# Casts of edge indices on ScalarE, sums cleared group by group, and a shorter Newton step in the head of a graph kernel

## The chip, the cores and the metric

The kernel runs on one core of one Trainium2 chip. The metric is the device time of one execution in microseconds (us). Engines are named as in the profile: PE (TensorE), DVE (VectorE), ACT (ScalarE), POOL (GpSimd), SP (SyncE, which here only issues DMAs).

## The reference

Two layers work on x, 12500 rows of 256. The first is a graph layer with 200000 edges, sorted by target; the second is graph attention with 131072 edges and a mixture of four experts.

```python
z = layernorm(x)
x = x + segment_sum(z[src] * edge_weight[:, None], dst) @ W.T + b
y = layernorm(x)
x = x + moe(y, scores=gat(y, edge_index))
```

LayerNorm is (x - mean) / sqrt(var + 1e-5) without scale and shift in the first layer.

## The kernel before

The 12500 rows are 98 tiles of 128 (NT); groups of 4 tiles (GT) make 25 groups (NG), the last of which has 2. The part that the change touches is the head, everything ahead of the loop over edges:

- Constants, then POOL clears acc_x, 99 tiles of 256 columns in which the sums of the first layer are collected, in 33 pieces of 3 tiles (L162, L163).
- SP loads src, dst and edge_weight as rows of 128 edges (L185 to L194, 1664 columns on each of 128 partitions with the rest row), then the first six groups of x (L213). The pool of x buffers has six (L171), so the load of a group must wait until the store of the group six before it has landed.
- `turned` (L196) turns each of the three so that an edge's chunk is a column: integers are first cast to float in place on DVE (L199), then 13 PE transposes in pieces of four into PSUM (L205), each piece copied out by ACT (L207). src goes to src1, dst to dst_f, the weights to w1.
- `windows` (L235 to L294) works out from dst_f which tiles of targets each window of 768 edges reaches, and splits the second layer's edge indices. It is some 30 instructions of DVE with a few of PE, and is called in the code when the statistics of group 8 have been issued.
- The LayerNorm loop (L298 to L316): for group g the statistics (L104, L105), var + EPS (L111) on DVE and the square root on ACT (L112); and for the group before, the Newton step that refines 1/root (L118 to L122, DVE), the offset -mean*r (L311, DVE), the normalisation of the tiles in place on ACT (L314), and the store to z_rows from ACT's queue (L316).
- W is loaded, turned on PE and ACT and stored (L321 to L328), all from memory that the x buffers and the head's scratch had; and L329 copies the first 5120 columns of the cleared acc_x to gat_starts, which thereby starts as zeros.

Then comes the loop over 261 windows (L581 to L605): POOL gathers 128 rows of z for each of 1563 chunks of edges (L550), DVE makes one-hot matrices, ACT scales them by w1 (L556), PE multiplies them with the gathered rows (L564), and DVE adds a window's sums to acc_x (L571). Beside it a counting sort of the second layer's edges runs on PE, DVE and ACT. The order of that loop is written out by hand for PE, DVE and ACT. In the head the framework puts the instructions of each engine in order, and not always in that of the code: in the trace L329 is issued ahead of all loads of x but the first six, and each store of z behind the first normalising instruction of the next group.

The Newton step of before, which the change rewrites, is

```python
nc.vector.reciprocal(r, s)
nc.vector.tensor_mul(s, r, r)
nc.vector.tensor_mul(s, s, v)
nc.vector.tensor_scalar(s, s, -0.5, 1.5, ALU.mult, ALU.add)
nc.vector.tensor_mul(r, r, s)
```

with v = var + EPS and s its root, cut to the tiles of the group.

Of the kernel before, what the change touches and what calls it, by code (L numbers as in the profile page):

```python
# [23 lines left out]
F32 = mybir.dt.float32  # L24
# [4 lines left out]
AF = mybir.ActivationFunctionType  # L29
ALU = mybir.AluOpType  # L30
# [4 lines left out]
P = 128  # L35
N, D = 12500, 256
NT = 98
# [15 lines left out]
GT = 4  # L53
NG = (NT + GT - 1) // GT
LOW = -1.0e30
CODE = 8192
EPS = 1e-5
# [3 lines left out]
def gnn_gat_moe(ctx, tc, x, src, dst, edge_weight, W, b, W_gat, att_src, att_dst, b_gat, ln_gamma,  # L61
                ln_beta, W1, b1, W2, b2, edge_index, out):
    nc = tc.nc
# [10 lines left out]
    def after_all(ins, others):  # L74

        for o in others:
            tc.add_manual_dep(ins.ins, o.ins.name, mybir.DependencyInfo(
                mybir.DependencyClass.Sync, mybir.DependencyReason.DATA),
                reason="one wait for what the next ones read")

    def rows_of(g):
        t0 = g * GT
        n = min(GT, NT - t0)
        return t0, n, min(N, (t0 + n) * P) - t0 * P

    def node_rows(table, t0, n):
        return table[t0 * P:(t0 + n) * P, :].rearrange("(t p) d -> p t d", p=P)

    def load_x(pool, g, eng):
        t0, n, rows = rows_of(g)  # L90
        full = rows // P
        xt = pool.tile([P, GT, D], F32, name="xt")
        eng.dma_start(xt[:, :full, :], node_rows(x, t0, full))
        if full < n:
            nc.vector.memset(xt[64:P, full, :], 0.0)
            eng.dma_start(xt[:TAIL, full, :], x[(t0 + full) * P:N, :])
        return xt

    def statistics(pool, xt, n):

        st = pool.tile([P, GT, 6], F32, name="st")
        mv = pool.tile([P, GT, 2], F32, name="mv")
        for i in range(n):
            nc.vector.bn_stats(st[:, i, :], xt[:, i, :])  # L104
            nc.vector.bn_aggr(mv[:, i, :], st[:, i, :])  # L105
        return mv, root(pool, mv[:, :n, 1], [P, GT], n)

    def root(pool, var, shape, n):
        v = pool.tile(shape, F32, name="v_eps")
        s = pool.tile(shape, F32, name="root")  # L110
        nc.vector.tensor_scalar_add(v[:, :n], var, EPS)  # L111
        nc.scalar.activation(s[:, :n], v[:, :n], AF.Sqrt)  # L112
        return v, s

    def rooted(pool, v, s, shape, n):

        r = pool.tile(shape, F32, name="rstd")
        nc.vector.reciprocal(r[:, :n], s[:, :n])  # L118
        nc.vector.tensor_mul(s[:, :n], r[:, :n], r[:, :n])
        nc.vector.tensor_mul(s[:, :n], s[:, :n], v[:, :n])  # L120
        nc.vector.tensor_scalar(s[:, :n], s[:, :n], -0.5, 1.5, ALU.mult, ALU.add)
        nc.vector.tensor_mul(r[:, :n], r[:, :n], s[:, :n])  # L122
        return r
# [35 lines left out]

    wide = tc.alloc_tile_pool(name="wide", bufs=1)  # L160
    acc_x = wide.tile([P, NT + 1, D], F32, name="acc_x")
    for k in range(0, NT + 1, 3):  # L162
        nc.gpsimd.memset(acc_x[:, k:k + 3, :], 0.0)  # L163
    with ExitStack() as s1:
        edges = s1.enter_context(tc.tile_pool(name="edges", bufs=1))
        small = s1.enter_context(tc.tile_pool(name="small", bufs=2))
# [18 lines left out]
        def chunk_load(ap, dt, name):  # L185
            t = prep.tile([P, full + 1, P], dt, name=name)
            nc.vector.memset(t[:, full, :], 0)
            nc.sync.dma_start(t[:, :full, :],
                              ap[0:full * P * P].rearrange("(k r e) -> r k e", r=P, e=P))
            at = full * P * P  # L190
            nc.sync.dma_start(t[:rest, full, :],
                              ap[at:at + rest * P].rearrange("(r e) -> r e", e=P))
            nc.sync.dma_start(t[rest:rest + 1, full, 0:left], ap[at + rest * P:E][None, :])
            return t  # L194

        def turned(t, into):  # L196
            if t.dtype != F32:
                f = t.bitcast(F32)
                nc.vector.tensor_copy(f, t)  # L199
                t = f  # L200
            for k0 in range(0, full + 1, GT):
                n = min(GT, full + 1 - k0)
                pp = ps.tile([P, GT, P], F32, name="look")
                for k in range(n):
                    nc.tensor.transpose(pp[:, k, :], t[:, k0 + k, :], ident)  # L205
                m = min(n * P, NQ * GQ - k0 * P)
                nc.scalar.activation(into[:, k0 * P:k0 * P + m],  # L207
                                     pp.rearrange("p k e -> p (k e)")[:, :m], AF.Copy)

        rows = [chunk_load(ap, dt, f"rows{k}") for k, (ap, dt) in enumerate(  # L210
            ((src, I32), (dst, I32), (edge_weight, F32)))]
        XB = 6
        early = [load_x(xp, g, nc.sync) for g in range(XB)]  # L213
        src1 = edges.tile([P, NQ * GQ], I32, name="src1")
        dst_f = prep.tile([P, NQ * GQ], F32, name="dst_f")
        w1 = edges.tile([P, NQ * GQ], F32, name="w1")
        for t, to in zip(rows, (src1, dst_f, w1)):
            turned(t, to)
        dst2 = prep.tile([P, NC2], I32, name="rows0")
        nc.sync.dma_start(dst2, edge_index[1].rearrange("(p c) -> p c", c=NC2))  # L220
        src2 = prep.tile([P, NC2], I32, name="rows2")
# [75 lines left out]
        ahead = None  # L297
        for g in range(NG + 1):  # L298
            done = ahead
            if g < NG:  # L300
                xt = early[g] if g < XB else load_x(xp, g, nc.sync)
                ahead = (g, xt, *statistics(small, xt, rows_of(g)[1]))
            if g == XB + 2:
                windows()
            if done is None:
                continue
            was, xt, mv, vs = done
            t0, n, _ = rows_of(was)
            r = rooted(small, *vs, [P, GT], n)
            off = small.tile([P, GT], F32, name="off")  # L310
            nc.vector.scalar_tensor_tensor(off[:, :n], mv[:, :n, 0], -1.0, r[:, :n], ALU.mult,  # L311
                                           ALU.mult)
            for i in range(n):
                nc.scalar.activation(xt[:, i, :], xt[:, i, :], AF.Identity, bias=off[:, i:i + 1],  # L314
                                     scale=r[:, i:i + 1])
            nc.scalar.dma_start(node_rows(Z, t0, n), xt[:, :n, :])  # L316
        sx.close()

        turning = s0.enter_context(tc.tile_pool(name="turning", bufs=1, reuse_waits="tile"))
# [240 lines left out]
        def product(rows, hots, there):  # L560

            win = ps.tile([P, D], F32, name="win")
            for j, (r, h) in enumerate(zip(rows, hots)):
                i = nc.tensor.matmul(win, h, r, start=(j == 0), stop=(j == len(rows) - 1))  # L564
                if j == 0:
                    after_all(i, there)
            return win
# [5 lines left out]
        def group(q):  # L573
            return prepare(src1, lo_q, w1, [c for c in range(q * GQ, (q + 1) * GQ) if c * P < E])
# [3 lines left out]
        with tc.manual_schedule(engines={mybir.EngineType.PE, mybir.EngineType.DVE,  # L578
                                         mybir.EngineType.Activation}):
            at, done, coming, win = (), 0, group(0), None  # L580
            for q in range(NQ + 1):  # L581
                was, win = win, product(*coming) if q < NQ else None
# [9 lines left out]
                if q < NQ and q % 4 == 0:  # L592
                    n = min(4, NQ - q)
# [3 lines left out]
                for work, q0, q1, steps in parts:  # L597
                    if q == q0:
                        done = 0
# [14 lines left out]
        with tc.If(further > 0):  # L614
# [9 lines left out]
            with tc.For_i(0, NQ, 1) as q:  # L624
                nc.vector.memset(shift, 0.0)
                n = nc.values_load(more[0:1, bass.ds(q, 1)], min_val=0, max_val=NT,
                                   skip_runtime_bounds_check_because=BOUND)
# [29 lines left out]
    with ExitStack() as s2:  # L657
        gp = s2.enter_context(tc.tile_pool(name="gp", bufs=3))
        small = s2.enter_context(tc.tile_pool(name="small2", bufs=3))
# [124 lines left out]
    with ExitStack() as s3:  # L784
# [20 lines left out]
        turned = []  # L805
# [52 lines left out]
        t = pre.tile([P, L2], F32, name="scan")  # L858
# [151 lines left out]
        def joined(m_in, s_in, m_own, name):  # L1010

            m = tail.tile([P, H], F32, name="m_" + name)
            nc.vector.tensor_max(m, m_in, m_own)
            f = tail.tile([P, 2, H], F32, name="f_" + name)
            nc.vector.tensor_sub(f[:, 0, :], m0, m)
            nc.vector.tensor_sub(f[:, 1, :], m_own, m)
            nc.scalar.activation(f, f, AF.Exp)
            return m, f
# [12 lines left out]
        _, f = joined(m_in, None, end[:, NS:], "end")  # L1031
# [13 lines left out]
        m, f = joined(m0, None, row[:, NS:], "row")  # L1045
# [7 lines left out]
    with ExitStack() as s4:  # L1053
# [118 lines left out]
        g, last = 0, None  # L1172
        for t0, t1 in ((0, 12), (12, 36), (36, 80), (80, NT)):
            with tc.issue_after(last.ins) if last else ExitStack():
                gates(t0, t1 - t0)
            while g * GT < t1:
                last = mixed(g)
# [26 lines left out]
```

## Time and profile before

| what | us |
|---|---|
| median of three runs | 4193.42 (4192.93 to 4193.94) |
| the profiled execution | 4198.22 |
| its span | 4196.4 |
| first root of LayerNorm (ACT) | 37.04 |
| first store of z (ACT's queue) | 41.76 |
| last store of z | 130.27 |
| first gather (POOL) | 141.18 |

Busy shares over the whole span: PE 85%, POOL 69%, DVE 57%, ACT 34%. The timeline lists instructions in order of their start, with duration, engine, line of the code, tiles written and read, and in brackets the idle time ahead of one and what ended it; SPq and ACTq are the queues from which SP and ACT issue DMAs, and equal neighbours are drawn together with their count. The stretches view gives busy time by engine between two points in time, then the granted PE clock, the DMA share and GB/s.

| stretch, us | DVE busy | ACT busy | POOL busy | DMA share | GB/s |
|---|---|---|---|---|---|
| 0 to 25 | 19.66 | 1.29 | 24.39 | 0.75 | 222 |
| 25 to 35 | 7.03 | 4.74 | 0.00 | 0.18 | 52 |
| 35 to 60 | 22.72 | 15.20 | 0.00 | 0.81 | 277 |
| 60 to 80 | 17.81 | 10.64 | 0.00 | 0.76 | 249 |
| 80 to 100 | 13.35 | 10.12 | 0.00 | 0.81 | 269 |
| 118 to 140 | 8.51 | 12.13 | 0.00 | 0.54 | 181 |

### The profile page before, as it was taken

Reading aid. Unit: us, or ns where it says so; the run is one execution under the profiler, and the core shown is the slowest. Engines: PE = TensorE matmul, PEld = TensorE weight load, DVE = VectorE, ACT = ScalarE, POOL = GpSimd, SP = SyncE. Lnnn points to the kernel's source line nnn. Section 1 sums busy time; section 2 is a strip of 40 time slices with the busy share of each in tenths; the row PEclk is TensorE's granted clock in tenths of the full one; section 3 lists DMA queues with packets and bytes.
Section 4 is the critical chain, followed back from the end, with each engine's and each line's share of the span. In section 5 each row is a group of like instructions: output and inputs, shape, how many; then the busy total and the mean of one; then the engine's idle time right before and its main releaser. Section 6 shows DMA issues by size and latency. Waiting matters only on the chain. (4 is left out here: it accounts for less than half of the span.)

```text
span 4196.4 us, 54596 instructions
## 1 busy us (share of the span) xinstructions
PE 3552.0 (85%) x18969; PEld 2610.1 (62%) x18970; DVE 2393.0 (57%) x5474; ACT 1421.4 (34%) x3289; POOL 2906.0 (69%) x2855
## 2 busy tenths in 40 slices
PE   1466899999999999999998959999989999899545
PEld 0365676767766667767677836666656666566424
DVE  7566777878787878787778950221211202212477
ACT  4322445445545444545452211221212212212122
POOL 2577777777777777777776777777777777773440
PEclk6688999999999999999999969999999999999767
DMA  7433333333333333333335652222222222221698
GB/s 234 135 93 93 102 102 100 100 100 101 100 101 100 99 101 101 100 101 100 99 102 157 191 145 60 67 72 55 64 50 75 75 55 64 65 60 62 206 226 346
DMA packets 265845, 457.42 MB, mean 109 GB/s; under 512 B 67943, under 2 KB 168705, under 8 KB 264289
## 3 DMA queue, kind: packets, MB, share of 16 engines
q0 software_dynamic: 114128, 219.11, 21.4%
q1 hardware_dynamic: 111663, 207.52, 14.0%
q10 hardware_dynamic: 39778, 27.28, 2.1%
q8 instruction: 153, 2.51, 0.2%
q14 instruction: 123, 1.01, 0.1%
HBM read 334.05 MB, written 119.66 MB: 108 GB/s over the span
## 5 line engine op out<-in xcount | busy, mean ns | idle before, releaser
L550 POOL DMA_INDIRECT gt<-z_rows,src x1563 | 1605.2, 1027 | 592.2 <-issue 410.2
L809 POOL DMA_INDIRECT G<-gat_nodes,order x1024 | 1026.5, 1002 | 339.3 <-issue 289.0
L564 PE MATMUL win<-gt,oh_w 128*128 128x256 f32 x3126 | 770.1, 398 | 200.4 <-DMA gt<-z_rows,src 149.3
L564 PEld LDWEIGHTS win<-gt,oh_w 128*128 128x128 f32 x3126 | 598.0, 198 | 317.0 <-issue 188.4
L966 PE MATMUL po<-w,hh 128*128 128x256 f32 x3136 | 724.3, 385 | 51.4 <-ACT hh L948 38.3
L966 PEld LDWEIGHTS po<-w,hh 128*128 128x128 f32 x3136 | 605.5, 193 | 220.8 <-issue 87.1
L970 DVE TENSOR_TENSOR fo<-po,b 128x512 f32<-128x512 f32 x196 | 135.3, 690 | 1016.6 <-PE po L966 1016.6
L942 PE MATMUL ph<-yt,w 128*128 128x512 f32 (+1 forms) x1600 | 707.8, 586 | 2.8 <-DMA w<-in_L_ffn_W 2.8
L556 ACT ACTIVATE oh_w<-hit_w,w 128x128 f32<-128x128 bf16 x1563 | 500.9, 390 | 448.2 <-PE win L564 226.6
L490 DVE TENSOR_SCALAR st<-along,place_l,code 128x1024 bf16<-128x1024 f16 x1024 | 550.3, 578 | 162.3 <-PE perm L498 161.7
L948 ACT ACTIVATE hh<-ph,b 128x512 f32<-128x512 f32 (+1 forms) x400 | 249.3, 676 | 1001.6 <-PE ph L942 1001.5
L498 PE MATMUL perm<-st,to_p 128*128 128x512 bf16 x2048 | 524.1, 378 | 0.0
L942 PEld LDWEIGHTS ph<-yt,w 128*128 128x128 f32 x1600 | 305.0, 191 | 292.5 <-issue 277.9
L454 PE MATMUL look<-next,oht 98*128 98x128 f32 x2044 | 393.8, 300 | 0.0
L454 PEld LDWEIGHTS look<-next,oht 98*128 98x128 f32 x2044 | 309.6, 192 | 37.5
L462 ACT ACTIVATE next<-place 98x256 f32<-98x256 f32 x511 | 196.1, 384 | 345.1 <-PE place L459 344.3
L469 DVE TENSOR_TENSOR sel<-look,oh_lo 128x512 f32<-128x512 f32 x256 | 174.9, 683 | 186.4 <-PE look L454 185.2
L498 PEld LDWEIGHTS <-to_p 128*128 128x128 bf16 x2048 | 178.5, 97 | 122.3 <-DVE st L490 0.4
L571 DVE SCALAR_TENSOR_TENSOR acc_x<-win,in,acc_x 128x256 f32 x522 | 246.9, 473 | 8.7 <-PE win L564 8.6
L450 PE MATMUL look<-oh_lo,same_hi 128*128 128x128 bf16 x1024 | 228.1, 223 | 1.2 <-ACT next L462 1.0
L442 ACT ACTIVATE same_hi<-bank 128x512 bf16<-128x512 f32 x256 | 152.8, 597 | 215.2 <-PE bank L440 215.1
L340 DVE TENSOR_TENSOR oh_hi<-twice,hi 128x784 bf16<-128x784 bf16 x256 | 143.4, 560 | 100.6 <-PE place L364 100.5
(278 smaller groups left out, 3641.8 us busy)
## 6 DMA issues: line engine op xcount, KB each, us to landing
expert_rows<-fo SPq DMA_DIRECT2D x48, 1024.0 KB, 4.2
fo_in<-expert_rows SPq DMA_DIRECT2D x24, 2048.0 KB, 16.4
gt<-z_rows,src POOLq DMA_INDIRECT x1563
G<-gat_nodes,order POOLq DMA_INDIRECT x1024
xt<-in_x SPq DMA_DIRECT2D x24, 512.0 KB, 4.8
z_rows<-xt ACTq DMA_DIRECT2D x24, 512.0 KB, 4.6
x_two<-in_x SPq DMA_DIRECT2D x12, 1024.0 KB, 6.4
x_rows<-x_two SPq DMA_DIRECT2D x12, 1024.0 KB, 10.6
```

The source lines that it names most:

```text
L450: first = nc.tensor.matmul(look[:, i % GT + k, :], b["m"][:, i + k, :], one(b["ol"], i + k), start=True, stop=False)
L454: nc.tensor.matmul(look[:, i % GT + k, :], b["oht"][:, i + k, :], nxt[:, k, :], start=False, stop=True)
L490: last = nc.vector.tensor_scalar(st[:, k, :], along, b["l"][:, i + k:i + k + 1], code2[:, c:c + 1], ALU.is_equal, ALU.mult)
L498: first = nc.tensor.matmul(perm[:, h, :], one(b["p"], i + k), st[:, k, h * 512:(h + 1) * 512], start=(c == 0), stop=(c == NC2 - 1), skip_g ...
L550: there = [nc.gpsimd.indirect_dma_start(out=rows[j], out_offset=None, in_=Z, in_offset=IND(ap=idx[:, c:c + 1], axis=0)) for j, c in enumer ...
L556: there += [nc.scalar.activation(hots[j], one(hit, j), AF.Copy, scale=w[:, c:c + 1]) for j, c in enumerate(chunks)]
L564: i = nc.tensor.matmul(win, h, r, start=(j == 0), stop=(j == len(rows) - 1))
L571: return nc.vector.scalar_tensor_tensor(to, win, m, to, ALU.mult, ALU.add)
L809: i = nc.gpsimd.indirect_dma_start(out=G[:, t + 1, :], out_offset=None, in_=NODE, in_offset=IND(ap=order[:, t:t + 1], axis=0))
L942: i = nc.tensor.matmul(ph[:, :n], w_1[:, e, k, f * P:(f + 1) * P], yts[g][:, :n, k, :], start=(k == 0), stop=(k == 1))
L948: i = nc.scalar.activation(item["hh"][:, f, :n * P], ph[:, :n].rearrange("p t m -> p (t m)"), AF.Gelu, bias=b_1[:, e * NF + f:e * NF + f + 1])
L966: m = nc.tensor.matmul(po[:, a, :], item["hh"][:, f, i * P:(i + 1) * P], w_2[:, e, f, :], start=(f == 0), stop=(f == NF - 1))
```

## The change

The clears leave the start. Behind the normalisation of each LayerNorm group POOL now clears as many tiles of acc_x as the group has (the last group the rest), with a wait for the last normalising instruction of that group. The two casts of edge indices go from DVE to ACT. The Newton step is two instructions behind the square of r: (var + EPS) * r^2, then (that - 3) * r, which leaves r times -2; so z is -2 times what it was, and w1 is taken out of PSUM with a scale of -1/2 in return. The square root adds EPS through its bias operand, so the add on DVE goes.

```diff
-    for k in range(0, NT + 1, 3):
-        nc.gpsimd.memset(acc_x[:, k:k + 3, :], 0.0)
...
-        def turned(t, into):
+        def turned(t, into, scale=1.0):
             if t.dtype != F32:
                 f = t.bitcast(F32)
-                nc.vector.tensor_copy(f, t)
+                nc.scalar.activation(f, t, AF.Copy)
...
                 nc.scalar.activation(into[:, k0 * P:k0 * P + m],
-                                     pp.rearrange("p k e -> p (k e)")[:, :m], AF.Copy)
+                                     pp.rearrange("p k e -> p (k e)")[:, :m], AF.Copy,
+                                     scale=scale)
...
-        for t, to in zip(rows, (src1, dst_f, w1)):
-            turned(t, to)
+
+        for t, to, by in zip(rows, (src1, dst_f, w1), (1.0, 1.0, -0.5)):
+            turned(t, to, by)
+        eps = edges.tile([P, 1], F32, name="eps")
+        nc.vector.memset(eps, EPS)
...
-                ahead = (g, xt, *statistics(small, xt, rows_of(g)[1]))
+                n = rows_of(g)[1]
+                st = small.tile([P, GT, 6], F32, name="st")
+                mv = small.tile([P, GT, 2], F32, name="mv")
+                for i in range(n):
+                    nc.vector.bn_stats(st[:, i, :], xt[:, i, :])
+                    nc.vector.bn_aggr(mv[:, i, :], st[:, i, :])
+                s = small.tile([P, GT], F32, name="root")
+                nc.scalar.activation(s[:, :n], mv[:, :n, 1], AF.Sqrt, bias=eps)
+                ahead = (g, xt, mv, s)
...
-            r = rooted(small, *vs, [P, GT], n)
+
+            r = small.tile([P, GT], F32, name="rstd")
+            nc.vector.reciprocal(r[:, :n], s[:, :n])
+            nc.vector.tensor_mul(s[:, :n], r[:, :n], r[:, :n])
+            nc.vector.scalar_tensor_tensor(s[:, :n], mv[:, :n, 1], EPS, s[:, :n], ALU.add, ALU.mult)
+            nc.vector.scalar_tensor_tensor(r[:, :n], s[:, :n], 3.0, r[:, :n], ALU.subtract, ALU.mult)
...
-                nc.scalar.activation(xt[:, i, :], xt[:, i, :], AF.Identity, bias=off[:, i:i + 1],
-                                     scale=r[:, i:i + 1])
+                last = nc.scalar.activation(xt[:, i, :], xt[:, i, :], AF.Identity,
+                                            bias=off[:, i:i + 1], scale=r[:, i:i + 1])
             nc.scalar.dma_start(node_rows(Z, t0, n), xt[:, :n, :])
+
+            clear = nc.gpsimd.memset(acc_x[:, t0:t0 + (n if was + 1 < NG else NT + 1 - t0), :], 0.0)
+            after_all(clear, [last])
```

More of the change, by code (lines that the diff above doesn't have):

```diff
@@ L306, in gnn_gat_moe @@
                 continue
-            was, xt, mv, vs = done
+            was, xt, mv, s = done
             t0, n, _ = rows_of(was)
-            r = rooted(small, *vs, [P, GT], n)
+            r = small.tile([P, GT], F32, name="rstd")
[3 more added lines that the diff above has]
+            nc.vector.scalar_tensor_tensor(r[:, :n], s[:, :n], 3.0, r[:, :n], ALU.subtract, ALU.mult)
             off = small.tile([P, GT], F32, name="off")
```

## The prediction

> **What bounds the kernel now.** I read the page first for the large shape, then the timeline of the first 145 us, the busy time by stretches, and SP's own queue. On the page the long middle is paced by the gathers and the matmuls beside them; the groups of instructions show the gathers, and the slices show what stands ahead of them.
>
> ```profile
> DVE  7566777878787878787778950221211202212477
> POOL 2577777777777777777776777777777777773440
> L550 POOL DMA_INDIRECT gt<-z_rows,src x1563 | 1605.2, 1027 | 592.2 <-issue 410.2
> ```
>
> POOL works at 2 tenths in the first slice and 5 in the second (a slice is 105 us), and at 7 from then on: the 1563 gathers of L550 are its work until about 2260 us, and they begin when z is in memory. So whatever ends the head (loads, LayerNorm, stores of z) sooner starts them sooner. Nothing in the change touches an instruction behind the head, so a shift of the head is a shift of the end.
>
> The timeline of the start is the view on which the rest stands (start, duration, engine, line, what idled ahead of it):
>
> ```profile
> 2.49 22.50 POOL L163 MEMSET acc_x<- 128x768 f32 x33
> 6.55 19.33 DVE L199 CAST rows<-rows 128x1664 f32<-128x1664 int32 x1 [4.41 <-DMA rows<-in_src]
> ...
> 26.85 1.01 DVE L199 CAST rows<-rows 128x1664 f32<-128x1664 int32 x1
> 27.09 0.60 ACT L207 ACTIVATE src<-look 128x512 int32<-128x512 f32 x1 [25.04 <-PE look L205]
> ...
> 35.58 0.38 SPq L329 DMA_DIRECT2D gat_starts<-acc_x  x1
> 35.74 1.28 ACT L112 ACT_TABLE_LOAD   x1
> 37.04 0.20 ACT L112 ACTIVATE root<-v_eps 128x4 f32<-128x4 f32 x1
> ```
>
> The same cast takes 19.33 us the first time and 1.01 the second. The first ends at 25.88; the 33 clears end at 24.99. So it ran for about 1 us once POOL was done, and for 18.3 us it stood. Everything hangs on it: transposes, ACT's copies, the first square root at 37.04, the first store of z at 41.76. DMA moves 6 GB/s from 20 to 24 us and nothing from 24 to 28.
>
> From there to the last store the head is a loop over six x buffers. One group's way round, by the timeline of SP, DVE and ACT: load of group 17 issued 90.54, its statistics 96.43, its normalisation 107.49, its store 110.33, and the load of group 23 into the same buffer 113.97.
>
> ```profile
> 105.38 0.43 DVE L104 BATCH_NORM_STATS2 st<-xt 128x6 f32<-128x256 f32 x1 [3.28 <-DMA xt<-in_x]
> ...
> 106.91 0.15 DVE L121 TENSOR_SCALAR root<-root 128x4 f32<-128x4 f32 x1
> 107.10 0.16 DVE L122 TENSOR_TENSOR rstd<-rstd,root 128x4 f32<-128x4 f32 x1
> 107.30 0.16 DVE L311 SCALAR_TENSOR_TENSOR off<-mv,rstd 128x4 f32<-128x4 f32 x1
> 107.49 0.60 ACT L314 ACTIVATE xt<-xt,off,rstd 128x256 f32<-128x256 f32 x1 [3.81 <-DVE off L311]
> ```
>
> The statistics here are group 19's, the Newton step among them group 17's: the normalisation stands two groups behind the statistics, and the store one more. So of 23.43 us for six groups three group periods (8.95 + 2.84 us) are waiting for neighbours, and 5.89 + 2.11 + 3.64 = 11.64 us is fixed (load to statistics, statistics to normalisation, store to next load). 6T = 3T + 11.64 gives T = 3.88 us a group, which is what the trace has. DMA is not full: 273 GB/s from 80 to 119 us, with bursts of 380 and gaps of 40 to 90. Between 40 and 76 us another limit rules: DVE is busy without a break there, with the windows' preparation (L242 to L294) between the groups.
>
> **The change, part by part.**
>
> 1. *Clears out of the start, casts on ACT.* The src rows are there at 6.55. ACT's cast of 1664 columns has no row. ACT's copies give two points: 128x512 at 0.597 us (L442) and 98x256 at 0.384 (L462), so 0.83 ns a column and 0.17 us fixed, thus 1.55 us. Lower end: 1.01, VectorE's. Upper end: L314 passes 256 columns from SBUF to SBUF in 0.52 us by its spacing, so 3.4 us. I take 1.55, since a copy is the nearest kind. The first cast then ends at 8.1 in place of 25.88. From the cast's end to the first root the trace has 37.04 - 25.88 = 11.16 us of transposes, copies and a table load, all of which stay; the second cast now stands in ACT's line too, +1.55 (less if it falls into ACT's first wait for PE). Root: 8.1 + 11.16 + 1.55 = 20.8. **-16.2 us**; 3.7 less at the upper price, 1.5 more if the second cast is hidden. Is x there? The first six loads were issued from 8.31 and DMA had drained them by 20 us, so group 0's statistics can run from about 13: the root is late, not x.
>
> 2. *Newton step.* Per group two DVE instructions go (L111's add of EPS, and one of the three in L120 to L122); each was 0.15 us long. In the loop only the chain counts: the three dependent steps above stand 0.20 us apart, so one fewer takes 0.20 off the 11.64, a third of that off T, 0.07 us for 19 groups: 1.3 us. In the windows' stretch each step waits behind an instruction of 0.94 to 1.78 us (group 3's six steps run from 46.14 to 52.68), one fewer saves about 1 us there, of which a part is hidden. **-1.5**, from 0 to -3.
>
> 3. *Clears in the loop.* 24 of 1024 columns and one of 768; 768 take 0.728, so 1024 take 0.97. POOL is idle from 25 to 141, so POOL itself pays nothing, and the last clear (behind the last ACT instruction, 129.64 to 130.24) ends about 131, 10 us ahead of the first gather, which waits for the weights' store (138.10) anyhow. But the 19.33 us row says that a clear can hold up a DVE instruction. No row shows statistics or four-column products beside a clear. Within the windows' stretch, where DVE has no idle time, five clears fall (groups 2 to 6): at most 4.9 us; elsewhere DVE has over 1 us idle a group (13.35 busy of 20 us from 80 to 100). **+1.5**, from 0 to 4.9. By the Trainium skill, "SBUF — State Buffer", section "Who interferes with whom", casts, copies and tensor_scalar in a two-port mode are held by a GpSimd instruction for its whole length, and one with a single input outside these modes is not. By that rule only the windows' casts and tensor_scalars can meet a clear, and the two instructions removed per group include both tensor_scalars; the stalled cast agrees, the rest no run here shows yet.
>
> 4. *The copy of cleared sums to gat_starts (L329, 2560 KB).* It now needs five groups' clears. Today it goes out at 35.58, in a gap of the DMA, and costs the first store little: from 41.76 to the load that waits for it, 47.41, are 5.65 us where 4.5 is usual for a store, so 1.2 is given back. It moves to behind the fifth normalisation (57.0 today) and its clear, between the loads of groups 9 and 10 (57.93 and 63.27). At 422 GB/s, the best stretch of today's copy, it takes 6.2 us. DMA was at 0.57 and 0.55 from 52 to 60, and the loads of groups 9 and 10 have 4.3 and 2.4 us to spare (issue + 4.8 against statistics at 67.07 and 70.48). I take 2 there: **+0.8** net, from -1.2 to +5.0. In a sentence by itself: the Trainium skill, "DMA: Bandwidth & Descriptors", section "Issuing engines are not separate DMA queues", has all issuers share the same 16 engines, which would make that the dearer end.
>
> 5. *Scales -1/2, memset of eps, square root with a bias:* immediates and operands of instructions that are there already; nothing. The tail from the last store (130.27) to the first gather (141.18), W's turning, stays as it is.
>
> Sum: -16.2 - 1.5 + 1.5 + 0.8 = **-15.4 us**. The profiled execution took 4198.22 (span 4196.4 and 1.8 around it); it would be 4182.8. The median of the runs is 4193.42, 4.8 below the profiled one; I take the sum off it: **4178 us**.
>
> **The rivals.**
>
> *A. Full prices.* Clears 4.9, copy +5.0, casts at 3.4 us each (+3.7): -16.2 - 1.5 + 4.9 + 5.0 = -7.8 with casts as taken, 4185.6, and -4.1 with all, 4189. For it: DVE has no slack from 40 to 76. Against: DMA has.
>
> *B. The lag grows (slower).* The change alters what is ready when on ACT, and the order of ACT and DVE is planned. If the normalisation falls three groups behind the statistics, 6T = 4T + 11.64 and T = 5.82: 1.94 us more for each of the 12 groups from 77 us on, and for perhaps half of the 7 ahead of them (16 in all, 31 us). -15.4 + 31 = +16, 4209. It decides from 0.96 us a group on (15.4 / 16). For it: the lag is already two where the code asks for one. Against: the root needs one DVE step fewer, so it comes sooner.
>
> *C. The lag shrinks.* With one group 6T = 2T + 11.64 and T = 2.91, just above 1.05 MB at 380 GB/s (2.76): 0.97 less for 12 to 16 groups, -12 to -16 more: about 4164. For it: same reason as against B. Against: ACT's root still stands behind four normalisations (root at 103.50, they end there).
>
> *D. The stall isn't the clears.* Then the start stays, and only parts 2 to 4 are left: +0.8, no change, 4194. Against: cast end and clears' end agree within 1 us.
>
> **How the numbers follow.** Forecast 0.62; A 0.14; B 0.09; C 0.12; D 0.03. A measurement of this kernel tells about 0.2%, 8.4 us, from no change. Forecast and C are faster; of A a small part. Faster 0.75, same 0.16, slower 0.09. The range takes C's price and A's: 4164 to 4189; it leaves out B, D and the outer part of C.
>
> **What would show it.** Right: L199 on ACT at about 6.6 for 1.5 us, first root near 21, first store of z near 25, first gather near 126, the middle as long as before. Step 3 is wrong if windows' instructions show durations of 1 us above today's; step 4 if statistics of groups 10 and 11 wait long for x behind L329; B and C show in the spacing of the stores. The prediction is wrong if the head's end does not follow its start.

## The result, and the profile after

The changed kernel takes 4175.5 us (median of five runs, 4170.96 to 4178.82) against 4193.92 us of the kernel before (4192.93 to 4196.18). The ratio is 0.9955 with an interval of 0.9941 to 0.9968, so 13 to 25 us less; 15.4 less, 4178 us, were forecast. The profiled execution has a span of 4177.0 us.

The timeline of the start of the changed kernel (start, duration, engine, line, idle time ahead and what ended it; lines behind the head are 18 higher than before):

```profile
6.23 1.28 ACT L197 ACT_TABLE_LOAD   x1 [6.11 <-DMA rows<-in_src]
7.52 3.07 ACT L197 ACTIVATE rows<-rows 128x1664 f32<-128x1664 int32 x2
10.50 1.28 ACT L205 ACTIVATE src<-look 128x512 int32<-128x512 f32 x2
...
18.46 1.28 ACT L311 ACT_TABLE_LOAD   x1
19.76 0.30 ACT L311 ACTIVATE root<-mv,eps 128x4 f32<-128x4 f32 x1
19.96 0.66 ACT L205 ACTIVATE w<-look 128x512 f32<-128x512 f32 x2
...
24.05 0.39 ACTq L331 DMA_DIRECT2D z_rows<-xt  x1
24.07 0.95 POOL L333 MEMSET acc_x<- 128x1024 f32 x1 [21.54 <-ACT xt L329]
```

The stall of 18.3 us is gone: the first root stands at 19.76 instead of 37.04. Two things are new. ACT's first table load, at 0.77 before, now stands behind the wait for the src rows. And the root was put ahead of the last two copies of the weights (L205, w), behind which it stood before.

The end of the head, from the timeline of the changed kernel:

```profile
115.02 0.37 ACTq L331 DMA_DIRECT2D z_rows<-xt  x1
117.79 0.37 SPq L339 DMA_DIRECT2D w_in<-in_L_gnn_W  x1
...
122.98 0.37 SPq L346 DMA_DIRECT2D w_turned<-w_out  x1
...
126.06 1.51 POOL L568 DMA_INDIRECT gt<-z_rows,src  x1 [10.28 <-DVE oh_hi L358]
```

The first gather comes 15.1 us sooner (141.18 before), and the tail from the last store to it is as long as it was (11.0 against 10.9). From the first gather to the end it is 4050.9 us against 4055.2. That difference is not the change's: a second profile of either kernel gave 4054.5 (changed) and 4047.1 (before), and 14 profiles of this study, all with the same code behind the head, lie between 4044.6 and 4056.0. So the total of one execution cannot tell differences of a few us, and the experiments are read from the head of their traces. There the second profiles put the first gather at 124.6 (changed) and 142.1 (before): the head got 16 us shorter, give or take one.

The window in which part of the gain was given back, in the changed kernel's queues of SP (loads of x and the copy to gat_starts) and ACT (the store of group 5):

```profile
39.61 0.37 SPq L93 DMA_DIRECT2D xt<-in_x  x1
40.07 0.55 SPq L347 DMA_DIRECT2D gat_starts<-acc_x  x1
40.86 0.37 SPq L93 DMA_DIRECT2D xt<-in_x  x1
...
41.48 0.37 ACTq L331 DMA_DIRECT2D z_rows<-xt  x1
...
52.92 2.01 SPq L93 DMA_DIRECT2D xt<-in_x  x2
```

The load of group 11 (52.92) had to wait for the store of group 5, which ACT issued at 41.48. The DMA view of the stretch from 40 to 48 us says why (q1 is SP's queue, q10 ACT's; packets, MB, share of 16 engines):

```profile
q1 hardware_dynamic: 624, 2.49, 81.3%
q10 hardware_dynamic: 43, 0.04, 1.5%
```

While the copy drained, two stores of 512 KB had been issued and moved 0.04 MB together. From 46 to 49 us the same view reads:

```profile
q1 hardware_dynamic: 54, 1.11, 85.6%
q10 hardware_dynamic: 55, 0.06, 5.3%
```

Packet for packet the two queues were then level, but one of the copy held about 20 KB and one of a store about 1 KB. The second profile of the changed kernel shows the same (60 and 58 packets, 1.23 and 0.06 MB). Why the stores moved almost nothing before 46 us, this does not show.

### The profile page after: what moved, and what is told of

Same layout as the page of the kernel before. It is cut to its first block, busy times and chain, and to the rows that moved or that the text cites. A ratio compares the mean times of both kernels' runs of the same rounds, so it can differ in the third digit from the quotient of the medians.

```text
span 4177.0 us, 54551 instructions
## 1 busy us (share of the span) xinstructions
PE 3548.8 (85%) x18969; PEld 2611.0 (63%) x18970; DVE 2371.0 (57%) x5423; ACT 1424.9 (34%) x3291; POOL 2902.0 (69%) x2847
```

## The experiments

Each differs from the kernel named by the edit shown. "Period" is the mean time from one store of z to the next from group 10 to group 20; "rest" is from the first gather to the end of the span; the ratio is to the kernel before, timed on the same chip.

| kernel | first root | period | first gather | rest | ratio (interval) |
|---|---|---|---|---|---|
| before | 37.04 | 3.91 | 141.2 | 4055.2 | 1 |
| before, again | 37.75 | 3.92 | 142.1 | 4047.1 | |
| changed | 19.76 | 3.77 | 126.1 | 4050.9 | 0.9955 (0.9941 to 0.9968) |
| changed, again | 19.75 | 3.52 | 124.6 | 4054.5 | |
| e1, before + casts on ACT | 28.80 | 4.05 | 135.5 | 4055.2 | 0.9981 (0.9973 to 0.9990) |
| e2, before + late clears | 19.46 | 4.08 | 128.8 | 4052.4 | 0.9967 (0.9954 to 0.9980) |
| e4, changed, old Newton step | 22.43 | 4.15 | 132.5 | 4049.4 | 0.9962 (0.9948 to 0.9976) |
| e9, e4, stores ahead | 21.47 | 4.20 | 132.8 | 4056.0 | 0.9988 (0.9979 to 0.9997) |
| e3, changed, first clears on DVE | 18.73 | 3.59 | 120.3 | 4052.7 | 0.9952 (0.9939 to 0.9965) |
| e5, changed, casts on DVE | 17.21 | 3.58 | 123.7 | 4052.9 | 0.9966 (0.9953 to 0.9978) |
| e6, changed, table early | 19.61 | 3.41 | 124.0 | 4051.8 | 0.9963 (0.9950 to 0.9977) |
| e7, e3 + e5 + e6 | 17.49 | 3.76 | 120.6 | 4044.6 | 0.9959 (0.9946 to 0.9973) |
| e8, changed, one step more | 18.68 | 3.67 | 123.7 | 4049.8 | 0.9963 (0.9952 to 0.9975) |
| e10, changed, stores later | 19.73 | 3.92 | 125.6 | 4048.5 | 0.9962 (0.9948 to 0.9975) |

**e1: the casts alone.** Two casts go to ACT, the clears stay at the start.

```diff
-                nc.vector.tensor_copy(f, t)
+                nc.scalar.activation(f, t, AF.Copy)
```

> The kernel before with nothing but its two casts moved to ScalarE; the 33 clears stay at the start. Port theory (the stream of clears holds up casts and tensor_scalars of DVE, whichever they are): DVE's casts and tensor_scalars of the constants (L131 to L151) now meet the clears and stand until about 25 us, the statistics behind them start at about 26, the first root comes at 28 instead of 37.0, the first gather at about 132, the whole 9 us shorter than before. Rival (it only matters that ACT does the cast): first root at 20, first gather at 125, 16 to 18 us shorter.

The root came at 28.80. DVE's timeline in e1:

```profile
2.06 22.99 DVE L136 CAST freeb<-free 128x128 bf16<-128x128 f32 x1
2.14 22.98 DVE L131 CAST identb<-ident 128x128 bf16<-128x128 f32 x1
25.05 0.26 DVE L141 TENSOR_SCALAR after<-free,part 128x128 f32<-128x128 f32 x1
```

A cast of 128 columns, 0.21 us in the kernel before, now shows 22.99: it takes over the stall from the cast that left. The theory holds as far as the runs reach: the stream of clears is the cause, and the first DVE cast that meets it pays. That a port is the means, no trace shows. The first gather came at 135.5 instead of the 132 expected; the total is 4 to 11 us shorter.

**e2: the clears alone.** The casts stay on DVE, the Newton step is the old one.

```diff
-    for k in range(0, NT + 1, 3):
-        nc.gpsimd.memset(acc_x[:, k:k + 3, :], 0.0)
...
+            clear = nc.gpsimd.memset(acc_x[:, t0:t0 + (n if was + 1 < NG else NT + 1 - t0), :], 0.0)
+            after_all(clear, [last])
```

> The kernel before with nothing but the clears moved behind the LayerNorm groups; casts on DVE, old Newton step. Port theory: the first cast takes 1.0 us and ends at 7.6, the first root comes at 18.7, the first gather at 126 to 129 and the whole is 12 to 17 us shorter than before. Rival (the cast is slow on DVE for another reason, ScalarE is needed): the cast still takes 19 us, first gather at 141 and no gain.

DVE's timeline in e2:

```profile
6.80 1.03 DVE L197 CAST rows<-rows 128x1664 f32<-128x1664 int32 x1 [4.67 <-DMA rows<-in_src]
...
9.51 1.03 DVE L197 CAST rows<-rows 128x1664 f32<-128x1664 int32 x1 [0.62 <-DMA rows<-in_dst]
```

1.03 us each, root at 19.46, first gather at 128.8: the late clears alone bring 12.4 of the head's gain, with no help from ACT.

**e4: the old Newton step.** In the changed kernel the square root takes var + EPS from DVE again, and the old step stands behind it.

```diff
+                v = small.tile([P, GT], F32, name="v_eps")
+                nc.vector.tensor_scalar_add(v[:, :n], mv[:, :n, 1], EPS)
-                nc.scalar.activation(s[:, :n], mv[:, :n, 1], AF.Sqrt, bias=eps)
+                nc.scalar.activation(s[:, :n], v[:, :n], AF.Sqrt)
...
+            r = rooted(small, *vs, [P, GT], n)
```

> The changed kernel with the old Newton step (var + EPS on DVE, then four instructions, z and w1 unscaled); casts on ScalarE and late clears stay. Newton theory: 1.5 to 4 us slower than the changed kernel, first gather at 127.5 to 130, with the loss in the windows' stretch and 0.07 to 0.2 us a group behind it. Rival (DVE waits for x anyhow): first gather at 126, the same time.

It lost 6.4 us of the head (132.5), more than either theory had. 2.7 are lost by the first root (22.43): 0.6 because the src rows landed later in this profile (ACT's first table load at 6.86 against 6.23), most of the rest because the root stands behind all copies of the weights again, as before. The loss is 5.9 by the store of group 10 (72.14 against 66.25) and 9.7 by that of group 20 (113.61 against 103.94), of which 3.3 come back in the last groups. e4 and e2 differ only in the engine of the casts, and e4's head is 3.7 us longer: with the clears out of the way ACT looks the worse place for them (e5 asks again).

**e8: one Newton instruction more.** EPS stays in the bias, the step gets its third instruction back.

```diff
-            nc.vector.scalar_tensor_tensor(r[:, :n], s[:, :n], 3.0, r[:, :n], ALU.subtract, ALU.mult)
+            nc.vector.tensor_scalar(s[:, :n], s[:, :n], -0.5, 1.5, ALU.mult, ALU.add)
+            nc.vector.tensor_mul(r[:, :n], r[:, :n], s[:, :n])
```

> The changed kernel with one Newton instruction more per group ((var + EPS) r^2, then times -1/2 plus 3/2, then times r; z and w1 unscaled), while EPS stays in the bias of the square root. The old step in full gave first gather 132.5 against 126.1. If the length of the chain on DVE makes these 6.4 us, half of them or more come back here: 129 to 131. If the add of EPS on DVE and the order that ScalarE's instructions get with it (root behind the last copies of the weights, stores one normalising instruction later) make them: 126 to 127.5.

First gather at 123.7, sooner than either theory had it: the longer chain costs nothing that can be seen. So the shorter chain is not what the Newton edit gained. The timeline of e8 shows something else, though:

```profile
77.11 0.95 POOL L334 MEMSET acc_x<- 128x1024 f32 x1 [2.68 <-ACT xt L330]
77.16 0.93 DVE L324 TENSOR_SCALAR root<-root 128x4 f32<-128x4 f32 x1
...
80.65 0.95 POOL L334 MEMSET acc_x<- 128x1024 f32 x1 [2.58 <-ACT xt L330]
80.76 0.16 DVE L322 TENSOR_TENSOR root<-rstd 128x4 f32<-128x4 f32 x1
80.95 0.16 DVE L323 SCALAR_TENSOR_TENSOR root<-mv,root 128x4 f32<-128x4 f32 x1
81.15 0.47 DVE L324 TENSOR_SCALAR root<-root 128x4 f32<-128x4 f32 x1
```

A tensor_scalar of four columns, 0.15 us before, takes 0.93 beside a clear, until the clear ends (seven of the 25 are held, 3.5 us in all, and the head is no longer for it); the two instructions ahead of it at 80.76 and 80.95, also beside a clear, take 0.16 as ever. By the Trainium skill, "SBUF — State Buffer", section "Who interferes with whom", an instruction with two inputs in SBUF meets only a GpSimd instruction that reads SBUF, and a tensor_scalar may enter a mode that any meets; the trace agrees in both, down to four columns.

**e9 and e10: the order of the stores.** In the changed kernel ACT issues a store directly behind its group's normalisation; in the kernels with the old step it stands behind the first normalising instruction of the next group. e9 gives e4 the first order, e10 gives the changed kernel the second.

```diff
+            with tc.issue_after(stored.ins) if stored else ExitStack():
...
-            nc.scalar.dma_start(node_rows(Z, t0, n), xt[:, :n, :])
+            stored = nc.scalar.dma_start(node_rows(Z, t0, n), xt[:, :n, :])
```

```diff
+                if i == 0 and waiting:
+                    store = nc.scalar.dma_start(*waiting)
+                    behind(store, last)
+            waiting = node_rows(Z, t0, n), xt[:, :n, :]
```

> The kernel with casts on ScalarE, late clears and the old Newton step (first gather 132.5), with ScalarE told to issue each store of z ahead of the next group's normalisation, as the changed kernel does of itself. Store theory (the old order holds each store back by most of a group; that, and not the instructions saved, is what the Newton edit gained in the loop): the period from group 10 to 20 falls from 4.15 to 3.4 to 3.8 us as in the kernels with the bias in the square root, first gather at 127 to 129. Rival (the add of EPS and the chain on DVE): period stays at 4.0 to 4.2, first gather at 131 to 133.

> The changed kernel, with each store of z put behind the first normalising instruction of the next group, as it stands in the kernel before. Store theory: the period from group 10 to 20 rises from 3.77 to 4.0 to 4.2 us, first gather at 129 to 132. Rival: period 3.6 to 3.8, first gather at 124 to 127.

e9 stayed at 132.8 and a period of 4.20, e10 at 125.6. The store theory falls as an account of the head's end, though the period in e10 rose to 3.92, that of the old order. It falls by e10: e9 moved more than the store, since there the root ahead of a store is that of three groups later, in the changed kernel of two. This root waited for the add of EPS, and the store behind it waited as well:

```profile
79.37 0.20 ACT L313 ACTIVATE root<-v_eps 128x4 f32<-128x4 f32 x1 [2.07 <-DVE v_eps L312]
79.43 0.37 ACTq L330 DMA_DIRECT2D z_rows<-xt  x1
```

What is left is the add of EPS between the statistics and the root, and a pair of runs has it alone: e4 and e8 both have five instructions in the step and an unscaled z, and e8 lacks only the add (EPS goes into the root's bias and into the product with r squared). First gather 132.5 with the add, 123.7 without. The whole gain of the Newton edit, 6.4 us here and 5.1 between e2 and e5, which differ in that edit alone, goes with this one instruction. How it costs so much is not shown: it takes 0.17 us a group, and clears hold it only twice in e4, for under 1 us in all. The framework's order changes with it, on ACT (the root's and the store's place) and on DVE: at 73 us in e4 the steps from the reciprocal to the offset stand between another group's statistics (73.63 to 75.47), in e8 they follow one another (73.80 to 74.79). No run keeps the add and changes only that order.

The totals are a coarse witness here: e4 and e9, whose first gathers are 0.2 us apart, have ratios whose intervals do not meet (0.9948 to 0.9976, 0.9979 to 0.9997), and nothing in the traces of the head says why.

**e3: the copy to gat_starts early.** The first 20 tiles are cleared by one memset on DVE at the start, the others as in the changed kernel.

```diff
+        nc.vector.memset(acc_x[:, 0:5 * GT, :], 0.0)
...
+            if was >= 5:
-            clear = nc.gpsimd.memset(acc_x[:, t0:t0 + (n if was + 1 < NG else NT + 1 - t0), :], 0.0)
-            after_all(clear, [last])
+                clear = nc.gpsimd.memset(acc_x[:, t0:t0 + (n if was + 1 < NG else NT + 1 - t0), :], 0.0)
+                after_all(clear, [last])
```

> The changed kernel, but the first 20 tiles of acc_x, which L329's copy reads, are cleared by one DVE memset at the start (5.3 us, ahead of the landing of x), so that the copy goes out before the loads of groups 6 and on. Copy theory (its 2560 KB among the loads cost the 6.5 us that groups 7 to 9 lost): first gather at about 120, the whole 4 to 6 us below the changed kernel. Rival (the windows' instructions on DVE cost them): first gather at 125 to 127, the whole as the changed kernel.

The SP queue of e3, and its DMA view from 19 to 27 us:

```profile
18.98 0.38 SPq L349 DMA_DIRECT2D gat_starts<-acc_x  x1
31.19 0.38 SPq L93 DMA_DIRECT2D xt<-in_x  x1
```

```profile
q1 hardware_dynamic: 515, 3.34, 105.0%
```

The copy now runs in a stretch in which the changed kernel moved 1.61 MB with 1.5 us of standstill, and the head is 5.8 us shorter (120.3; 4.3 against the second profile). The gain lies where the theory put it: the store of group 9 comes at 59.23 instead of 63.65, although those of groups 0 to 6 are within 1.2 us. The copy theory holds for the head; e3 also takes the first five clears off POOL, but beside those five no DVE instruction of the changed kernel shows a hold above 0.03 us. That the whole would be 4 to 6 us shorter does not show: the ratio is 0.9952 against 0.9955.

**e5, e6 and e7: the casts back, the table early, all three.** e5 undoes the edit of e1 in the changed kernel; e6 adds a square root of one column at the start.

```diff
+        warm = edges.tile([P, 1], F32, name="warm")
+        nc.vector.memset(warm, 1.0)
+        nc.scalar.activation(warm, warm, AF.Sqrt)
```

> The changed kernel with its two casts back on DVE. From the runs so far: with late clears and the old Newton step the casts on ScalarE made the head 3.7 us longer (first gather 132.5 against 128.8), since two casts and a table load of 1.28 us stand in ScalarE's line ahead of the first copy. Theory: ScalarE's casts lose about as much here, first root at 16.5 to 17.5 instead of 19.8, first gather at 122 to 123.5. Rival (casts off DVE help because DVE has its hands full): first gather at 126 or later.

> The changed kernel with a square root of one column on ScalarE at the very start, so that the table load does not stand behind the wait for the src rows, and the square root's set is there for the whole head (one load instead of two). Theory: the two loads at 6.23 and 18.46 are both on the way to the first root, root at 17.2 to 17.6 instead of 19.8 and first gather at 123.5 to 125. Rival (statistics of x, not ScalarE, hold the root): root as before, first gather 126.

> The changed kernel with casts on DVE, the first 20 tiles cleared by DVE at the start, and the early table load: the three that cost it least, together. If they add up: first gather at 126.1 - 3.7 - 5.8 - 1.3 = 115 to 117, the whole 9 to 11 us below the changed kernel. If the loop over x has a floor of its own (DMA 21.4 MB of x and z from the first store on at the 380 GB/s of its bursts is 56 us, the trace's gaps make it 90): first gather at 118 to 120.

e5: root at 17.21 as expected, first gather at 123.7, 2.4 us sooner than the changed kernel and 0.9 sooner than its second profile; the direction is that of e2 against e4, the size is at the edge of the spread. e6: the loads are gone from the way, but the root then stands behind all copies of the weights and comes at 19.61, so it did not do what was expected; its first gather at 124.0 was forecast, but not for this reason, and lies within the spread. e7: 120.6, later than both of its theories had it and no better than e3 alone. The three do not add up. Both e3 and e7 beat the changed kernel's head by 4 to 6 us, but not by a time that the totals can tell: their ratios, 0.9952 and 0.9959, lie in its interval.

**The repeats.**

> The changed kernel again, for the spread of one profile of the head: first gather within 2 us of 126.1 if the differences of 3 us and more between the kernels are theirs.

> The kernel before again, for the same: first gather within 2 us of 141.2, and the time from there to the end within 6 us of 4055.

Both expectations held except for the time behind the gather of the kernel before, 4047.1, 8 us off.

## Why the prediction came true, step by step

- **The stall is the clears' (right).** e1 and e2 show it from both sides. Rival D (the stall isn't the clears) is out.
- **Step 1, casts and start: 17.3 instead of 16.2, by two errors that cancel.** The casts were priced well (3.07 for two, 3.1 forecast). The first table load (1.28, behind the wait for src) was not seen: the first cast ended at 9.11 instead of 8.1. Neither was that the root would be put ahead of two copies: from there to the root it is 10.65 us instead of 12.71. That place comes with the Newton edit; without it (e4) the root stands at 22.43, and clears and casts alone bring 14.6, less than forecast. That "casts on ACT" are part of the gain was an assumption nobody had asked for: the clears alone bring the root to 19.46, and ACT's casts cost 1 to 4 us (0.9 to 2.4 by e5, 3.7 by e4 against e2).
- **Step 2, Newton: -5.1 to -6.4 instead of -1.5, for another reason.** e4 and the pair e2, e5 give the size, e8 refutes the working (one step of 0.20 us fewer per period). What failed is "in the loop only the chain counts": e4 against e8 puts the gain on the add of EPS, which the prediction counted as one of two instructions of 0.15 us. The term was mis-sized by 3.6 to 4.9 us.
- **Step 3, clears in the loop: about 0.1 instead of 1.5.** Of the windows' casts only one shows a hold, 0.42 us where 0.29 is usual (L260); where a clear came second, it was the clear that waited:

```profile
34.75 0.97 DVE L253 TENSOR_SCALAR scratch<-rows 128x1566 f32<-128x1566 f32 x1
...
34.91 1.70 POOL L333 MEMSET acc_x<- 128x1024 f32 x1 [4.78 <-ACT xt L329]
```

  POOL has time for that. e8 shows that the removal of both tensor_scalars avoids such holds, for the one put back is held in the loop; the head of e8 is no longer for it, so they cost nothing there.
- **Step 4, the copy: 4.3 to 5.8 instead of +0.8.** The place was right (between the loads of groups 9 and 10), the upper end was right (5.0). The loads of groups 9 and 10 did have time to spare (DVE waited 0.7 us for group 9 and not at all for group 10). What failed is that nothing else was priced: the prediction looked at the loads in SP's queue and not at ACT's stores beside the copy, and a late store is a late load six groups on (DVE waited 1.5 us for group 11 and 1.7 for group 12).
- **Step 5 and the tail (right).** 11.0 against 10.9 us. The root with its bias takes 0.09 us more, which was put at nothing and cannot be seen in the head.
- **Sum.** -15.4 forecast, -15.1 and -17.5 in the head of two pairs of profiles, -18.4 in the medians. Without the Newton edit's share in step 1 the measured parts (14.6, 5.1 to 6.4, 0.1 and 4.3 to 5.8) add up to -13.8 to -16.6, about what the heads show. Steps 2 and 4 were off by 3.5 to 5 us each, in opposite directions: the mechanism of the start was right, but that the sum came out this close was luck.
- **Rivals.** B and C did not come: the root at 78.09 serves the Newton step at 80.98, still two groups behind the statistics, and the period is 3.52 to 3.77 instead of 3.91. The store's lag did shrink, which no rival had: it now follows its normalisation directly (of group 17, from 91.91, store at 94.01), 2.1 us behind its start where 2.84 were before. A came in its copy term only.

## What to carry to other kernels

Look first for an instruction whose duration is far from that of its twin, and ask which other engine's stream ended when it did: the cure is to break the stream up, not to move the instruction, for the next one of its kind inherits the stall. When a transfer moves, list what is issued on every other queue while it drains; a store that feeds a ring of buffers is paid for one round later. A sum can be right with parts that are wrong, so test the terms alone before reusing them.

## What the runs showed of the hardware that was not expected

A DVE cast that is issued 0.43 us ahead of the first clear (e1, 2.06 against 2.49), while a POOL iota runs (1.56 to 2.53), never gets in between the 33 clears that follow, and its whole wait of 22.8 us is shown as its duration, not as idle time. A square root with its bias in memory takes 0.28 to 0.30 us against 0.19 to 0.20 without; the Trainium skill, "ScalarE: Activation LUTs", section "What ACT_TABLE_LOAD costs", has about 93 ns for each such operand, and the trace agrees. And a large copy on one hardware queue can leave almost nothing to stores issued on another while it drains: 2.49 MB against 0.04 in 8 us, and in the last part, where the packets of the two were equal in number, 1.11 against 0.06, because the copy's were some 20 times larger.
